# Where a rotary exchange runs: block 1's halves by DMAs of SyncE instead of TensorE, and three stack transfers by GpSimd's queue

## The chip, the core and the metric

The kernel runs on one core of a Trainium2 chip. The metric is the device time of one execution in microseconds; the time before the change is the median of three runs. A profile of one execution shows every instruction on TensorE (PE, with its weight loads PEld), VectorE (DVE), ScalarE (ACT), GpSimd (POOL) and the DMA queue of SyncE (SP). All times below are microseconds (us) from the start of the profiled span unless they are marked ns.

## The reference

`x` is 2 x 2048 x 256, float32. It is normalized over its last axis; the result feeds causal attention (16 heads of 16, 4 key and value heads) and a spectral layer; both are added to `x`.

```python
xn = _layernorm(x, axis=-1)
q = (xn @ wq).reshape(Bx, Sx, 16, 16); k = (xn @ wk)...; v = (xn @ wv)...
def _apply_rope(t, cos, sin):
    t1, t2 = jnp.split(t, 2, axis=-1)
    return jnp.concatenate([t1 * cos - t2 * sin, t1 * sin + t2 * cos], axis=-1)
q = _apply_rope(q, cos, sin); k = _apply_rope(k, cos, sin)
scores = jnp.where(causal, jnp.einsum('bshd,bthd->bhst', q, k) / sqrt(16), -inf)
out = jnp.einsum('bhst,bthd->bshd', softmax(scores), v).reshape(Bx, Sx, 256) @ wo
y = real(ifft(einsum('bnd,do->bno', fft(xn), w))) + bias
return x + out + y
```

What the change touches is `_apply_rope`: each half of a head's features is multiplied by the cosine, and the other half, exchanged, by the sine.

## The kernel before

The 2 x 2048 rows are cut into 8 blocks of 512 rows (`NB`), in the order block row 0 of both sequences, block row 1 of both, and so on: blocks 0 and 1 are the first 512 rows of the two sequences. Each block has 4 units of 4 heads, so 32 units in all; unit u of block n has the queries of 4 heads.

**Preparing a block** (`project`, lines 425 to 637). The rows are normalized (`norm`), transposed on TensorE (`ps_x`, copied to `xnT`) and multiplied with the weights (`features`, tile `ps_q`, copied by ScalarE to `raw`). This is done in three chunks of 128 features: `c == NK` (chunk 2 in the tile names) holds keys and values, chunks 0 and 1 the queries of units 0 and 1, and 2 and 3. Features of a head's two halves lie 32 partitions apart, so the exchange of halves (`other_half`, lines 486 to 511) moves groups of 32 partitions. For blocks 0 and 1 (`n < 2`) it is a TensorE product with a permutation (`swap`, tile `ps_sw`). Block 0's rotation runs on VectorE, which reads the product from PSUM. Block 1's runs on GpSimd from SBUF, so ScalarE copies the product to `sw` (line 501). From block 2 on, DMAs of SyncE copy `raw` to `sw` (lines 506 to 511): two for the keys, four for a query chunk.

`rotate` makes `raw * cos`, `sw * sin` and their sum, `split` cuts the float32 result into three bfloat16 parts "h", "m" and "l" (lines 579 to 609), on VectorE for block 0 and on GpSimd for the others (line 429). The parts are stacked on partitions into `kst` (keys) and `qst` (a unit's queries), by `QPART = "hmlhmhm"` in seven pieces of 64 KB. For keys and for the very first unit `stack` sends these seven directly (`direct`, line 529); for the other units `stack_runs` writes the parts to a buffer in DRAM (`run`) and reads the stack back in three transfers. All of these go through `later`, which puts them on SyncE's queue in one stream per block.

**The main loop.** For each unit the maxima of the score rows are taken first: TensorE computes scores (`sd` for the diagonal, `sm` for earlier blocks), VectorE reduces them (`top_g`, `mx`, then `np_of`, lines 686 to 815). `spread` (lines 817 to 830) turns the negated maxima by TensorE (`ps_m`), copies them on ScalarE to `mt`, and a DMA from ScalarE's queue appends them to the unit's `qst`. Only then can TensorE compute the transposed scores (`st`, or `sp` at the end), ScalarE their exponentials (`es`, line 952), and TensorE the product with the values (`av`). Later come the division by the sums and the output (`po`).

**What sets the order.** The order on every engine is written by the kernel's own planner while the kernel is built (lines 1344 to 1464). It keeps an estimated clock for each engine (`use`, line 127) and each DMA queue (`send`, line 141), with costs written into the code, and pieces of work in streams, each with what it needs and when it is due. It always takes the piece that its clocks say can start soonest, with preferences by kind (maxima, scores, values, fillers). Fillers are, among others, the six pieces of the spectral matrix (`spectral_matrix`, lines 361 to 410): four `ps_ff` and two `ps_mff`. Each engine then executes its instructions strictly in the planned order, waiting on semaphores. So a cost or a need that is changed in one place can move work anywhere.

Of the kernel before, what the change touches and what calls it, by code (L numbers as in the profile page):

```python
# [23 lines left out]
def tile_attn_plus_spectral_ffn(  # L24
# [29 lines left out]
    nc = tc.nc  # L54
# [3 lines left out]
    DH = 16  # L58
# [9 lines left out]
    NK = D // P  # L68
# [3 lines left out]
    QPART = "hmlhmhm"  # L72
# [20 lines left out]
    ring, used = {}, {}  # L93
# [6 lines left out]
    def take_slot(tag):  # L100
        used[tag] += 1
        return used[tag] - 1
# [24 lines left out]
    def use(eng, us, needs=(), gives=()):  # L127
        clock[eng] = max(clock[eng], ready(needs)) + us
        if eng == "pe":
            at = issued[0] // LOADED  # L130
            for k in range(max(loaded), at + 1):
                clock["pe"] = max(clock["pe"], loaded[k])
                loaded[k + 1] = clock["pe"] + LOAD
            clock["pe"] = max(clock["pe"], loaded[at])
        for k in gives:
            there[k] = clock[eng] + LATE[eng]
# [4 lines left out]
    def send(eng, kb, needs, gives, late=0.1):  # L141


        mine = lane.setdefault(eng == "pool", [0.0] * LANES)
        clock[eng] = max(clock[eng], mine[0])
        clock[eng] = max(clock[eng], ready(needs)) + (0.75 if eng == "pool" else 0.62)
        moved[eng] = max(moved.get(eng, 0.0), clock[eng] + 1.5) + 0.008 * kb
        mine.append(moved[eng] + 0.1)
        mine.pop(0)
        for k in gives:  # L150
            there[k] = moved[eng] + late
# [10 lines left out]
    def through_bank(us, needs, eng, eng_us, gives, eng_needs=()):  # L162

        k = take_slot("st")
        use("pe", us, (*needs, ("st", k - ring["st"])), [("ps", k)])
        use(eng, eng_us, (("ps", k), *eng_needs), [("st", k), *gives])
# [18 lines left out]
    def load_x(n):  # L185
# [31 lines left out]
        out=mask, in_=mask, pattern=[[-1, P]], compare_op=ALU.is_ge, fill=NEG, base=0,  # L217
# [6 lines left out]
        out=mask_t, in_=mask_t, pattern=[[1, P]], compare_op=ALU.is_ge, fill=NEG, base=0,  # L224
# [12 lines left out]
    for q in range(0, P, QD):  # L237
# [11 lines left out]
        out=rows_g[:, :, 0:3], in_=rows_g[:, :, 0:3], pattern=[[0, 2 * NKV], [-QD, 3]],  # L249
# [3 lines left out]
        out=rows_g[:, :, 38:41], in_=rows_g[:, :, 38:41], pattern=[[0, 2 * NKV], [QD, 3]],  # L253
# [48 lines left out]
    wp = const.tile([P, NK, NC, P], F32, name="wp")  # L302
# [122 lines left out]
    def project(n):  # L425
# [5 lines left out]
        raw, sw, swp, part, ra, at, held = {}, {}, {}, {}, {}, {}, {}  # L431
        sends = []
        streams.append(sends)

        def later(out, in_, kb, needs, gives):


            def go():
                nc.sync.dma_start(out=out, in_=in_)
                send("sp", kb, needs, gives)  # L440

            sends.append((-1, -1, "sp", needs, [], go))

        def norm(i):
            e.tensor_scalar(
# [19 lines left out]
        def features(c, k):  # L465
            if k == 0:
                held[c] = bank(f"ps_q{n}_{c}"), take_slot("st")
            ps, at_st = held[c]
            product(ps, wp[:, k, c, :], xnT[n][:, k, :], start=(k == 0), stop=(k == NK - 1))
            use("pe", 0.9, ["wp", ("xnT", n, k), ("st", at_st - ring["st"])], [("ps", at_st)])  # L470
            if k < NK - 1:
                return
            raw[c] = work.tile([P, SB], F32, tag="raw", bufs=3, name=f"raw{n}_{c}")
            at[c] = take_slot("raw")
            nc.scalar.copy(raw[c], ps)  # L475
            use(
                "act", 0.48, [("ps", at_st), ("raw", at[c] - ring["raw"])],
                [("st", at_st), ("raw", "in", n, c)],
            )
            if n >= 2:  # L480
                other_half(c)

        def rows(c):
# [2 lines left out]
        def other_half(c):  # L486
            sw[c] = work.tile([P, SB], F32, tag="sw", bufs=3, name=f"sw{n}_{c}")
            at[c, "sw"] = take_slot("sw")
            free = ("sw", at[c, "sw"] - ring["sw"])
            if n < 2:  # L490
                ps = bank(f"ps_sw{n}_{c}")
                product(ps, swap, raw[c], start=True, stop=True)
                if n == 0:
                    swp[c] = ps
                    at[c, "st"] = take_slot("st")
                    use(
                        "pe", 0.95, [("raw", "in", n, c), ("st", at[c, "st"] - ring["st"])],
                        [("sw", "in", n, c)],
                    )
                else:  # L500
                    nc.scalar.copy(sw[c], ps)
                    through_bank(
                        0.95, [("raw", "in", n, c)], "act", 0.48, [("sw", "in", n, c)], [free]
                    )
                return
            for base in range(0, rows(c), HP):
                one, two = slice(base, base + QD), slice(base + QD, base + HP)
                last = [("sw", "in", n, c)] if base + HP == rows(c) else []
                needs = [("raw", "in", n, c), free]
                later(sw[c][one, :], raw[c][two, :], 64, needs, [])  # L510
                later(sw[c][two, :], raw[c][one, :], 64, needs, last)
# [19 lines left out]
        def stack(c, a_part, f):  # L531
            src = part[c][f * HP : (f + 1) * HP, "hml".index(a_part), :]
            for a in range(len(QPART)):
                if (KPART if c == NK else QPART)[a] == a_part:
                    to = kst[n] if c == NK else qst[n, 2 * c + f]
                    gives = []
                    if a == len(QPART) - 1 if c == NK else a_part == "l":
                        gives = [("kst", n) if c == NK else ("stk", n, 2 * c + f)]
                        gives += [("part", at[c, "part"])] * (c == NK)
                    needs = [("part", "in", n, c, a_part)]  # L540
                    later(to[a * DH : (a + 1) * DH, :, :], src, 64, needs, gives)

        def stack_runs(c, units):

# [34 lines left out]
        def split(c, k):  # L579
# [23 lines left out]
            else:  # L603
# [7 lines left out]
        xs = [("xnT", n, k) for k in range(NK)]  # L611
        pe = [
            ("pe", [("xn", n, i) for i in range(NI)], ["st"] + ["xnT"] * (c == 0),
             lambda c=c: transpose_x(c))
            for c in range(NK)
        ]
        for c in (NK, 0, 1):
            table = [("cs", j, 1)] * (n >= 2)
            pe.append(("pe", ["wp", *table, xs[0]], ["st", "raw"] + ["sw"] * (n >= 2), lambda c=c: features(c, 0)))
            pe.append(("pe", [xs[1]], [], lambda c=c: features(c, 1)))  # L620
            if n < 2:
                pe.append(("pe", [("raw", "in", n, c)], ["st", "sw"], lambda c=c: other_half(c)))
            if c == NK:
                pe.append(("pe", [("raw", "in", n, NK), ("ones", n)], ["st"], proj_v))
# [572 lines left out]
    for u in range(len(units)):  # L1197
        at = max(0, first[u] - AHEAD[blocks[units[u][0]][1]])
# [317 lines left out]
```

## Time and profile before

| | |
|---|---|
| median of 3 runs | 898.05 us (897.0 to 899.27) |
| profiled execution, its time | 896.71 us |
| profiled execution, its span | 895.0 us |
| TensorE idle in the span | 895.0 - 879.4 = 15.6 us |
| `sw<-raw` DMAs | 60, 64 KB each |
| `res<-avs` issues of GpSimd's queue | 30, 600 ns each, 2.8 us to landing |

The span runs from the first instruction to the last; the execution's own time is 1.7 us longer. The page divides the span into 40 slices of 22.4 us; a digit is the busy share of a slice in tenths:

```profile
PE   8899999999999999999999999999999999999998
DVE  7987987798988996899888899979889889798501
POOL 8868558836932335611356321212652011101111
DMA  5554623441432012520012510010142001100000
```

TensorE is busy throughout. VectorE and GpSimd are as busy as TensorE only in the first 100 us, where blocks 0, 1 and 2 are prepared beside the first units. The granted TensorE clock was 1.0 throughout.

In the lists of instructions below each row gives the start, the length, the engine, the line, the operation, the tiles written and read, how many instructions were joined, and in brackets the idle time of the engine before it and what ended it. A product of the code is twice as many rows of float32 matmuls in the profile: the four matmuls of one `ps_sw` are eight rows.

### The profile page before, as it was taken

To read this page: it belongs to the slowest core of one execution; us is meant where nothing else is said; L and a number is where in the kernel's file an instruction comes from. 1 tells how busy PE (TensorE), PEld (TensorE's weight loads), DVE (VectorE), ACT (ScalarE), POOL (GpSimd) and SP (SyncE) were. 2 spreads that over 40 slices of the span, in tenths; PEclk is the share of its full clock that TensorE was granted. 3 is DMA by queue.
4 is the path that set the end of the run, shared out by engine and by line. 5 is a ranking of instruction groups with operands and counts; after the bars stand their busy time and mean duration, and the time that the engine had idled before them with its cause. 6 is when DMAs were issued, how large, how long until landed. Compare 5 with 4: busy or idle time off the path is not lost.

```text
span 895.0 us, 37152 instructions
## 1 busy us (share of the span) xinstructions
PE 879.4 (98%) x16620; PEld 481.8 (54%) x16620; DVE 730.8 (82%) x1002; ACT 638.3 (71%) x1191; POOL 365.0 (41%) x491
## 2 busy tenths in 40 slices
PE   8899999999999999999999999999999999999998
PEld 5477664565565555555555555554455554545443
DVE  7987987798988996899888899979889889798501
ACT  4276747685857874877855977858598887579885
POOL 8868558836932335611356321212652011101111
PEclk9999999999999999999999999999999999999999
DMA  5554623441432012520012510010142001100000
GB/s 176 139 137 118 197 67 112 123 120 49 107 106 86 27 40 78 142 74 15 17 44 87 150 40 14 27 39 14 52 123 61 14 3 39 50 14 15 27 2 25
DMA packets 42063, 62.02 MB, mean 69 GB/s; under 512 B 8920, under 2 KB 32200, under 8 KB 41904
## 3 DMA queue, kind: packets, MB, share of 16 engines
q1 hardware_dynamic: 32480, 41.18, 17.1%
q0 software_dynamic: 8128, 17.69, 6.2%
q8 instruction: 130, 2.13, 1.0%
q10 hardware_dynamic: 1296, 0.79, 0.3%
q14 instruction: 29, 0.24, 0.1%
HBM read 32.75 MB, written 18.40 MB: 57 GB/s over the span
## 4 chain that ended last, share of the span: by engine, by line
PE 88%; DVE 7%; ACT 3%; DMA 1%; issue 1%; SPq 0%; ACTq 0%; DVEq 0%
PE av L121 25%; PE st L121 24%; PE sm L121 18%; PE sd L121 7%; PE po L121 6%; PE ps_q L121 4%; ACT es L952 2%; DVE top_g L681 2%; PE sp L121 2%; DVE mx L681 1%; DMA qst<-mt 1%; PE ps_x L125 1%; PE ps_m L121 0%; DMA trig<-rope_dram 0%; DVE np_of L808 0%
## 5 line engine op out<-in xcount | busy, mean ns | idle before, releaser
L952 ACT ACTIVATE es<-st 128x512 f32<-128x512 f32 x1006 | 532.3, 605 | 133.6 <-PE st L121 116.9
L681 DVE TENSOR_REDUCE mx<-sm 128x2 f32<-128x1024 f32 x384 | 450.1, 1217 | 41.4 <-PE sm L121 40.0
L121 PE MATMUL st<-qst,kst 115*32 115x512 bf16 (+8 forms) x4744 | 340.5, 345 | 1.3 <-DMA qst<-mt 0.5
L121 PE MATMUL av<-es,va 128*32 128x512 f32 (+3 forms) x2560 | 289.7, 529 | 0.7 <-ACT avs L1033 0.2
L121 PE MATMUL sm<-kst,qst 112*32 112x512 bf16 x3072 | 237.9, 379 | 1.5 <-DVE top_g L681 0.8
L121 PEld LDWEIGHTS <-kst 115*32 115x32 bf16 x5120 | 164.2, 95 | 139.2 <-issue 62.3
L121 PEld LDWEIGHTS <-qst 112*32 112x32 bf16 x5632 | 153.2, 96 | 129.9 <-issue 82.1
L681 DVE TENSOR_REDUCE top_g<-sd 128x25 f32<-128x800 f32 (+1 forms) x192 | 167.5, 905 | 34.9 <-PE sd L121 34.5
L970 POOL TENSOR_SCALAR_AFFINE_SELECT es<-es 128x512 f32<-128x512 f32 (+1 forms) x120 | 65.3, 547 | 228.2 <-ACT es L952 228.2
L121 PEld LDWEIGHTS av<-es,va 128*32 128x32 f32 x2560 | 82.8, 109 | 47.4 <-issue 18.0
L121 PE MATMUL sd<-kst,qst 112*32 112x384 bf16 (+11 forms) x2560 | 101.1, 256 | 2.6 <-DVE top_g L681 1.7
L1044 POOL DMA_DIRECT2D res<-avs x30 | 18.0, 600 | 118.5 <-ACT avs L1023 118.5
L121 PEld LDWEIGHTS <-ident_h 128*32 128x32 bf16 x1344 | 46.2, 95 | 22.8 <-issue 16.3
L1158 DVE TENSOR_TENSOR xr<-po,xr 128x256 f32<-128x256 f32 x36 | 15.2, 424 | 47.1 <-PE po L121 46.7
L121 PE MATMUL sd<-mask,ident_h 128*32 128x64 bf16 x1024 | 53.4, 193 | 0.1
L121 PE MATMUL ps_q<-xnT,wp 128*32 128x512 f32 x384 | 47.5, 594 | 0.2 <-ACT xnT L460 0.2
L475 ACT COPY raw<-ps_q 128x512 f32<-128x512 f32 x24 | 14.1, 586 | 44.9 <-PE ps_q L121 37.1
L952 ACT ACTIVATE es<-sp 128x1024 f32<-128x1024 f32 x41 | 39.7, 1027 | 6.1 <-PE sp L121 5.9
L566 POOL TENSOR_TENSOR ra<-raw,cs 128x512 f32<-128x512 f32 (+1 forms) x21 | 27.0, 1286 | 24.6 <-ACT raw L475 23.6
L121 PE MATMUL po<-wo_sb,attT 128*32 128x256 f32 x512 | 34.4, 380 | 0.0
L121 PE MATMUL po<-mff,xnT 128*32 128x256 f32 x512 | 33.9, 379 | 0.0
L827 ACT CAST mt<-ps_m 12x512 bf16<-12x512 f32 x32 | 18.3, 571 | 19.1 <-PE ps_m L121 18.6
(113 smaller groups left out, 615.9 us busy)
## 6 DMA issues: line engine op xcount, KB each, us to landing
qst<-run SPq DMA_DIRECT2D x62, 128.0 KB
res<-avs POOLq DMA_DIRECT2D x30, 256.0 KB, 2.8
run<-part SPq DMA_DIRECT2D x31, 192.0 KB
qst<-run SPq DMA_DIRECT2D x31, 192.0 KB
xr<-in_L_attn_x_dram SPq DMA_DIRECT2D x16, 256.0 KB
sw<-raw SPq DMA_DIRECT2D x60, 64.0 KB
attT<-res POOLq DMA_DIRECT2D x15, 256.0 KB, 4.2
inv<-sums POOLq DMA_DIRECT2D x15, 256.0 KB, 3.7
```

The costliest lines, as they stand in the source:

```text
L121: nc.tensor.matmul(to, lhsT, rhs, **more)
L125: nc.tensor.transpose(to, of, unit)
L475: nc.scalar.copy(raw[c], ps)
L566: e.tensor_tensor(ra[c][:r], raw[c][:r], cs[j][:r, 0, :], ALU.mult)
L681: nc.vector.tensor_reduce(out, of, AX.X, ALU.max)
L827: nc.scalar.copy(mt, ps[0 : 3 * NKV, :SB])
L952: nc.scalar.activation(to, of, AF.Exp, scale=SCALE)
L970: nc.gpsimd.affine_select(out=to, in_=to, pattern=pattern, compare_op=ALU.is_ge, fill=0.0, base=0, channel_multiplier=-1,)
L1044: nc.gpsimd.dma_start(out=res[n, c][f], in_=avs[u])
L1158: nc.vector.tensor_tensor(xr[n, r][:, e, :], po, xr[n, r][:, e, :], ALU.add)
```

## The change

Block 1's exchange no longer goes through TensorE and ScalarE: it uses the same DMAs of SyncE as block 2 and later blocks, ten transfers of 64 KB for its three chunks. Only block 0 keeps the product. The features of block 1 accordingly ask for a free `sw` buffer before they start.

In the direct stack of the first unit, the three "h" pieces of the seven are issued from GpSimd's queue, in a stream of their own; the planner's note that the stack is complete (`stk`) then also needs those three. The key stacks (`c == NK`) stay on SyncE.

```diff
-        def later(out, in_, kb, needs, gives):
+        sends_pool = []
+        streams.append(sends_pool)
+
+        def later(out, in_, kb, needs, gives, pool=False):
+
+            q, name = (nc.gpsimd, "pool") if pool else (nc.sync, "sp")
 
             def go():
-                nc.sync.dma_start(out=out, in_=in_)
-                send("sp", kb, needs, gives)
-
-            sends.append((-1, -1, "sp", needs, [], go))
+                q.dma_start(out=out, in_=in_)
+                send(name, kb, needs, gives)
+
+            (sends_pool if pool else sends).append((-1, -1, name, needs, [], go))
...
-            if n >= 2:
+            if n >= 1:
                 other_half(c)
...
-            if n < 2:
+            if n == 0:
                 ps = bank(f"ps_sw{n}_{c}")
                 product(ps, swap, raw[c], start=True, stop=True)
-                if n == 0:
-                    swp[c] = ps
...
-                else:
-                    nc.scalar.copy(sw[c], ps)
-                    through_bank(
-                        0.95, [("raw", "in", n, c)], "act", 0.48, [("sw", "in", n, c)], [free]
-                    )
+                swp[c] = ps
...
                     needs = [("part", "in", n, c, a_part)]
-                    later(to[a * DH : (a + 1) * DH, :, :], src, 64, needs, gives)
+                    by_pool = c < NK and a_part == "h"
+                    if by_pool:
+                        gives = [("stk h", n, a)]
+                    elif gives and c < NK:
+                        needs += [("stk h", n, k) for k in range(7) if QPART[k] == "h"]
+                    later(to[a * DH : (a + 1) * DH, :, :], src, 64, needs, gives, by_pool)
...
-            pe.append(("pe", ["wp", *table, xs[0]], ["st", "raw"] + ["sw"] * (n >= 2), lambda c=c: features(c, 0)))
+            pe.append(("pe", ["wp", *table, xs[0]], ["st", "raw"] + ["sw"] * (n >= 1), lambda c=c: features(c, 0)))
             pe.append(("pe", [xs[1]], [], lambda c=c: features(c, 1)))
-            if n < 2:
+            if n == 0:
                 pe.append(("pe", [("raw", "in", n, c)], ["st", "sw"], lambda c=c: other_half(c)))
```

The transfers that are used instead were in the code already:

```python
            for base in range(0, rows(c), HP):
                one, two = slice(base, base + QD), slice(base + QD, base + HP)
                last = [("sw", "in", n, c)] if base + HP == rows(c) else []
                needs = [("raw", "in", n, c), free]
                later(sw[c][one, :], raw[c][two, :], 64, needs, [])
                later(sw[c][two, :], raw[c][one, :], 64, needs, last)
```

More of the change, by code (lines that the diff above doesn't have):

```diff
@@ L489, in other_half @@
             free = ("sw", at[c, "sw"] - ring["sw"])
-            if n < 2:
+            if n == 0:
                 ps = bank(f"ps_sw{n}_{c}")
                 product(ps, swap, raw[c], start=True, stop=True)
-                if n == 0:
-                    swp[c] = ps
[L495 to L498, printed above, removed]
-                    )
-                else:
-                    nc.scalar.copy(sw[c], ps)
-                    through_bank(
-                        0.95, [("raw", "in", n, c)], "act", 0.48, [("sw", "in", n, c)], [free]
-                    )
+                swp[c] = ps
+                at[c, "st"] = take_slot("st")
+                use(
+                    "pe", 0.95, [("raw", "in", n, c), ("st", at[c, "st"] - ring["st"])],
+                    [("sw", "in", n, c)],
+                )
                 return
```

## The prediction

> **What bounds the kernel now.** I read the page first (busy shares and the chain that ended last), then busy time by stretches, then the instructions of TensorE, VectorE and GpSimd between 14 and 100 us, and last the waits of the SyncE queue.
>
> ```profile
> span 895.0 us, 37152 instructions
> PE 879.4 (98%) x16620; PEld 481.8 (54%) x16620; DVE 730.8 (82%) x1002; ACT 638.3 (71%) x1191; POOL 365.0 (41%) x491
> ...
> PE 88%; DVE 7%; ACT 3%; DMA 1%; issue 1%; SPq 0%; ACTq 0%; DVEq 0%
> ```
>
> TensorE is the bound: 88% of the chain, and 895.0 - 879.4 = 15.6 us of idle in all. So a change is worth the TensorE work it removes, minus the TensorE idle it makes. The stretches (span; PE, PEld, DVE, ACT, POOL busy; clock; DMA share) say where the idle lies:
>
> ```profile
> 20.00:30.00 10.00, 9.31 (x144) 4.21 (x140) 9.55 (x14) 3.47 (x7) 9.25 (x14) 1.00 0.36 106
> 30.00:40.00 10.00, 8.41 (x188) 4.75 (x184) 8.93 (x16) 2.46 (x5) 8.48 (x8) 1.00 0.49 135
> 40.00:50.00 10.00, 9.01 (x274) 6.87 (x271) 9.18 (x26) 6.69 (x14) 9.42 (x12) 1.00 0.73 178
> 80.00:100.00 20.00, 18.62 (x580) 12.44 (x571) 17.73 (x38) 13.82 (x28) 17.44 (x21) 1.00 0.65 189
> 500.00:600.00 100.00, 100.00 (x1833) 53.91 (x1829) 88.46 (x101) 76.93 (x147) 19.64 (x30) 1.00 0.16 47
> ```
>
> About 8 us of idle lie before 100 us, 2.0 between 100 and 800, 5.6 at the end. The changed instructions all lie between 17 and 45 us, where VectorE and GpSimd are over 85% busy too. The gaps there, and one removed product, in TensorE's order of time (start, length, what, idle before it):
>
> ```profile
> 29.16 0.31 PE L121 MATMUL sd<-kst,qst 112*32 112x32 bf16 x8 [0.69 <-DMA qst<-part]
> ...
> 32.27 0.35 PE L121 MATMUL sd<-kst,qst 112*32 112x384 bf16 x4 [1.45 <-DVE top_g L681]
> ...
> 35.84 1.02 PE L121 MATMUL ps_sw<-raw,swap 128*32 128x512 f32 x5
> 36.65 1.94 PE L121 MATMUL ps_q<-xnT,wp 128*32 128x512 f32 x16
> ...
> 43.90 0.38 PE L121 MATMUL st<-qst,kst 115*32 115x512 bf16 x4 [0.52 <-DMA qst<-mt]
> ```
>
> The first gap is the wait for the stack the change touches, the second a wait for VectorE, the third the trip of the first unit's negated maxima (`mt`).
>
> **What goes away.** Three products `ps_sw` of block 1. Start to next start: 26.01 to 26.99, 35.79 to 36.65, 39.38 to 40.26: 0.98 + 0.86 + 0.88 = 2.7 us of TensorE. Their three ScalarE copies (586 ns each, 1.8 us) go too, worth nothing: ScalarE is busy 2.46 of 10 us at 30 to 40.
>
> **What SyncE gets.** Ten transfers `sw<-raw` more, three stack transfers fewer.
>
> ```profile
> L439 SPq DMA_DIRECT2D sw<-raw x60: 507/588/1216, 65.2 to 645.6; - x60
> ```
>
> At 0.6 us an issue that is 10 x 0.6 - 3 x 0.6 = 4.2 us more on an in-order queue. I replay it in its new order. Three "m" transfers 23.5 to 25.3, two `sw` of the key chunk (its `raw` is there at 25.2) to 26.5, the "l" transfer to 27.1, run 1 to 27.8, four `sw` of chunk 0 (28.6, after its `raw`) to 31.0, two of chunk 1 to 32.3, unit 1's three stack reads to 34.5 (32.27 before), two runs to 35.7, two `sw` to 36.9, five key transfers to 40.0, units 2 and 3 to 43.1, two key transfers to 44.3. With 2.2 us to land (the first pair of block 2's `sw` was issued by 66.4, its user started at 68.71), unit 0's stack is complete at 29.3, as now; unit 1's at 36.7, needed at about 39.2; block 1's keys at 46.5, needed at 65. So nothing on this queue reaches TensorE; without the 2.5 us of cover at unit 1 its lateness would count one for one. Later, units 6 and 7 stand behind block 2's first `sw` pair (issued near 67 instead of 59 to 65); their maxima come near 84 us.
>
> **What GpSimd gets.** Three issues of 0.6 us (`res<-avs`: 600 ns) after the key memset that ends at 23.17, so 23.2 to 25.0, landing near 27: before the "l" part. Block 1's key chunk starts at 25.2 instead of 25.97, but a 2.6 us memset pair now stands inside it, so its second step comes 1.4 us later than 27.79. Then
>
> ```profile
> 37.57 1.29 POOL L569 TENSOR_TENSOR sw<-sw,cs 128x512 f32<-128x512 f32 x1 [1.06 <-DVE top_g L681]
> ```
>
> this wait for chunk 0's exchange goes (the transfer lands by 33.2), which returns 1.06. GpSimd's chain is within 0.4 us of today's from there on.
>
> These three issues are the part for which I have no row: GpSimd's issues beside VectorE's casts. The nearest row is VectorE's cast, 0.44 us alone and 1.38 us beside a GpSimd multiply:
>
> ```profile
> 21.80 0.44 DVE L590 CAST part<-raw 128x512 bf16<-128x512 f32 x1
> ...
> 26.34 1.38 DVE L590 CAST part<-raw 128x512 bf16<-128x512 f32 x1
> ```
>
> Bounds: nothing, or one such 1.38 us hold for each issue, 4.1 us. I take nothing: only one 0.45 us cast (23.00) falls into 23.2 to 25.0, and the memset there did not stretch it. The Trainium skill, "SBUF — State Buffer", on the shared port pair, speaks against this part: a GpSimd-issued DMA needs GpSimd to write descriptors, which a VectorE copy in a two-port mode locks out, about 620 ns becoming 3100; by that figure the three would cost 7.4 us more (an estimate from that page), which no run here shows yet.
>
> **What the new order does.** Taking a need off TensorE lets the kernel's own planner choose anew, and this outweighs the rest. Six pieces of the spectral matrix (four `ps_ff`, two `ps_mff`, 1.73 us each: 3.49 for two) now all stand ahead of unit 0's `ps_m`; before, two did, two came later, and both `ps_mff` at 73.75. Replay of TensorE: `ps_ff` until 26.0, `ps_v` 26.4, chunks 0 and 1 at 1.73 each to 29.9, `ps_ff` 31.6, two diagonal steps of 0.4 to 32.4, `ps_ff` 34.1, two to 34.9, `ps_ff` 36.7, two to 37.4, `ps_mff` 39.2, two of unit 1 to 39.9, `ps_mff` 41.6, `ps_m`.
> 1. The gaps of 0.69 and 1.45 close: -2.1.
> 2. `ps_m` starts at 41.6 instead of 39.25. From it to the first `st` takes 43.90 - 39.25 = 4.65, so that comes at 46.25: 2.35 later. Only three diagonal steps (1.3 us) are left to cover that trip, so some 2.9 us are idle, against 0.52: +2.4.
> 3. From there to unit 1's first `st` it was 54.46 - 43.90 = 10.56 with one `ps_ff`, so 8.8 without: 55.1. But unit 1's `mt` must have landed: VectorE ends unit 0's maxima at 40.6 (last reduction 39.0, closing steps 1.6), then 2 x 0.7 + 4 x 0.95 + four statistics 2.4 + closing 1.5 make 49.7; a free bank and the steps ahead of it put `ps_m` at 50.9, ScalarE's copy ends at 52.0 behind its exponentials, 3.6 more (40.29 to 43.86) is 55.6. I take 55.6: 1.15 later than now.
> 4. The order is then the same until `ps_mff` at 73.75, which is done already: 1.15 - 3.49 = 2.3 us ahead. What VectorE does next, however, waits for its own chain: unit 4's maxima end at 76.5 + 1.15 = 77.65, and
>
> ```profile
> 77.81 5.14 DVE L681 TENSOR_REDUCE top_g<-sd 128x18 f32<-128x576 f32 x6 [1.32 <-PE sd L121]
> ```
>
> starts 0.16 earlier, no more. From here to 99.7 VectorE idles only 0.25 + 0.97 + 0.52 = 1.7, so the stretch ends between 0.16 and 1.9 us earlier. I take the middle, **1.0 us earlier**: 2.7 saved, 1.7 returned as idle.
> 5. After 100 us the order differs in most places but the work is the same, at 99.5 to 100% busy; the last units have the same order. Bounds: the 2.0 us of idle there vanish, or as much again comes; I take 0.
>
> Sum: 895.0 - 1.0 = 894.0 of span, 895.7 for the profiled execution (896.7); the median of the runs is 1.3 above that one, so 898.05 - 1.0 = **897.1 us**.
>
> **Rivals.**
> *Faster: the saving stays.* The 2.7 and the two closed gaps (2.1) count, and the late `mt` is covered by what VectorE and ScalarE have ready: 898.05 - 4.8 = 893.3; with only the 2.3 us of step 4 and half of the later idle, 894.8. For it: TensorE has almost no slack anywhere else, so work removed should show. Against it: VectorE's 17.7 of 20 us at 80 to 100. Center 894.
>
> *Slower: the trips of `mt` lose their cover.* With all fillers spent by 42 us, each unit of blocks 0 and 1 has only its own maxima, scores and values to cover some 4.2 us from `ps_m` to `st`. The planner counts 0.62 + 1.5 + 0.1 us for that transfer (lines 146 and 147), the trace 3.6 to 4.45. Six more trips follow before 100 us. Two of them as bare as step 2 (2.4 each) decide it: -1.0 + 4.8 = 901.9. For it: unit 2's trip (4.45 us from 59.93) is on the chain already. Against it: the orders after unit 1 are alike.
>
> *GpSimd held up.* At the 4.1 us bound the "h" parts land near 31.2, just before TensorE asks at 31.6, but block 1's chain on GpSimd is some 3.0 late, and block 2's normalization, now 2 us further back in its order, ends near 56 when TensorE wants it at 53.9: +2.2, 899.3. By the skill's figure above it would be worse still.
>
> That the products stay cannot be: they are gone from TensorE's order.
>
> **How the numbers follow.** Forecast 0.38, saving stays 0.32, bare trips 0.25, GpSimd held up 0.05. 0.3% is 2.7 us, about what a measurement of this kernel can tell from no change: limits 895.4 and 900.7. The forecast's own range is 895.0 to 899.0; 0.04 of it falls faster, 0.01 slower; of the last rival 0.02 slower. Faster 0.32 + 0.04 = 0.36, slower 0.25 + 0.01 + 0.02 = 0.28, same 0.36. Range: from 892.5 (4.8 and part of the later idle) to 902.5 (a third trip partly bare).
>
> **What would show it.** Right: no gap near 29 or 31 us, a wait `st <- DMA qst<-mt` of 2 to 3 us near 43 to 46, `top_g` of unit 5 near 77.7, PE busy 2 to 3 us less. Wrong: that wait under 1 us (faster), several such waits (slower), GpSimd's three issues over 1 us each, or waits of `sd` for `qst<-run`.

## The result, and the profile after

The changed kernel takes 895.39 us (median of 7 runs, 894.41 to 899.34) against 898.05: 0.9976 of the time before, 95% interval 0.9965 to 0.9988, some 2.7 us at the median. That lies on the border that the prediction itself drew between no change and faster (895.4). A second set of runs, further down, gives 895.79 and 0.9961 [0.9946, 0.9975]. The profiled execution took 896.04 us, with a span of 894.3. The head of its page and the chain that ended last:

```profile
span 894.3 us, 37136 instructions
PE 876.2 (98%) x16596; PEld 476.2 (53%) x16596; DVE 729.0 (82%) x1002; ACT 637.0 (71%) x1188; POOL 365.6 (41%) x494
...
PE 92%; DVE 5%; ACT 2%; issue 1%; DMA 0%; POOL 0%; ACTq 0%; POOLq 0%
```

TensorE has 24 matmuls (the three products) and 3.3 us of busy time less (879.4 before). Its idle time is 894.3 - 876.2 = 18.1 us, some 2.6 more than before. The span shrank by 0.7 only: 3.3 saved, 2.6 returned. The same stretches as shown of before (span; PE, PEld, DVE, ACT and POOL busy; clock; DMA share; GB/s) tell where:

```profile
20.00:30.00 10.00, 10.00 (x109) 3.96 (x105) 9.45 (x15) 3.56 (x7) 9.31 (x16) 1.00 0.39 94
30.00:40.00 10.00, 10.00 (x288) 7.25 (x284) 5.84 (x9) 1.98 (x5) 8.98 (x9) 1.00 0.65 161
40.00:50.00 10.00, 7.07 (x200) 4.76 (x189) 9.35 (x27) 4.07 (x10) 9.47 (x10) 1.00 0.50 134
80.00:100.00 20.00, 18.72 (x590) 12.92 (x584) 18.74 (x39) 15.21 (x30) 18.62 (x22) 1.00 0.63 171
500.00:600.00 100.00, 99.87 (x1811) 54.80 (x1807) 88.72 (x102) 74.53 (x143) 18.51 (x28) 1.00 0.11 33
```

The gaps at 20 to 40 us (0.7 and 1.6) are gone, and 1.9 us more are idle at 40 to 50. Over longer stretches, idle before and after: 7.9 and 9.0 up to 100 us, 3.5 and 3.4 from 100 to 885, 4.2 and 5.7 from there to the end. The timeline of TensorE shows the idle of 40 to 50 us (start, length, what, idle before it and its releaser):

```profile
41.91 0.22 PE L121 MATMUL ps_m<-ident_h,np_of 128*12 128x128 bf16 x1
...
45.01 0.35 PE L121 MATMUL sd<-kst,qst 112*32 112x384 bf16 x4 [1.92 <-DVE top_g L684]
...
46.46 0.38 PE L121 MATMUL st<-qst,kst 115*32 115x512 bf16 x4 [0.83 <-DMA qst<-mt]
...
55.35 0.38 PE L121 MATMUL st<-qst,kst 115*32 115x512 bf16 x4
```

Between unit 0's `ps_m` and its first `st` only a few diagonal steps are left, so TensorE waits once for VectorE to free a bank and once for the trip of `mt`: 2.75 us. From 38 to 60 us there is one wait more, to which the profile gives no releaser ("issue"); it ends at 59.3 us, and the experiments come back to it:

```profile
PE sd L121 <- issue: 0.7, 1, 0.7
```

In VectorE's timeline, unit 5's first reduction starts where it did before (77.81):

```profile
77.70 5.10 DVE L684 TENSOR_REDUCE top_g<-sd 128x18 f32<-128x576 f32 x6
```

From 77 to 100 us VectorE now hardly waits for scores any more; first before, then after (the columns: total, times, longest):

```profile
DVE top_g L681 <- PE sd L121: 3.1, 4, 1.3
```

```profile
DVE top_g L684 <- PE sd L121: 0.6, 1, 0.6
```

GpSimd's timeline has the three issues, at 0.54 us each, and no wait before chunk 0's `sw` step:

```profile
23.57 1.63 POOL L443 DMA_DIRECT2D qst<-part  x3
...
38.27 1.29 POOL L572 TENSOR_TENSOR sw<-sw,cs 128x512 f32<-128x512 f32 x1
```

How far is the changed kernel ahead? ScalarE's copy of `mt` marks each unit. Unit 0 starts it at 42.43 instead of 39.68, unit 1 at 51.47 instead of 49.52, unit 5 at 84.91 instead of 85.06, unit 7 at 99.60 instead of 101.03, unit 28 at 717.36 instead of 719.93, and the last unit is 2.43 us earlier, as is the last piece of computation. That is 1.7 us more than the span shows. The rest lies behind the last computation, in SyncE's wait for the output to land; first after, then before:

```profile
SPq L1515 <- DMA out_dram<-xr: 3.1, 2, 2.8
```

```profile
SPq L1512 <- DMA out_dram<-xr: 0.9, 2, 0.5
```

In this execution one packet of instructions (16 KB) ran at 890.9 to 891.85, and 18 packets of the output came in one by one until 892.9.

### The profile page after: what moved, and what is told of

Read it like the earlier page. It is cut to its first block, busy times and chain, and to the rows that moved or that the text cites. A ratio compares the mean times of both kernels' runs of the same rounds, so it can differ in the third digit from the quotient of the medians.

```text
span 894.3 us, 37136 instructions
## 1 busy us (share of the span) xinstructions
PE 876.2 (98%) x16596; PEld 476.2 (53%) x16596; DVE 729.0 (82%) x1002; ACT 637.0 (71%) x1188; POOL 365.6 (41%) x494
## 4 chain that ended last, share of the span: by engine, by line
PE 92%; DVE 5%; ACT 2%; issue 1%; DMA 0%; POOL 0%; ACTq 0%; POOLq 0%
PE av L121 25%; PE st L121 24%; PE sm L121 18%; PE sd L121 7%; PE po L121 6%; PE ps_q L121 5%; DVE top_g L684 2%; PE sp L121 2%; ACT es L955 1%; PE idle L125 1%; PE ps_x L125 1%; DVE mx L684 1%; PE ps_ff L121 1%; DVE np_of L811 1%; PE ps_m L121 1%
## 5 line engine op out<-in xcount | busy, mean ns | idle before, releaser
L121 PEld LDWEIGHTS <-qst 112*32 112x32 bf16 x5632 | 150.4, 96 | 127.3 <-issue 81.9
L1072 POOL DMA_DIRECT2D sums<-den x15 | 8.0, 534 | 63.7 <-DVE den L1066 63.7
```

What stands on the lines that cost most here:

```text
L121: nc.tensor.matmul(to, lhsT, rhs, **more)
L1072: nc.gpsimd.dma_start(out=sums, in_=den[n, c])
```

## The experiments

Ratios are to runs of the kernel before on the same chip. A lead or lag of two kernels with the same order was read at the same matmul of TensorE, counted from the start.

**1. The parts, and the order.** The change does three things at once: it takes the products away, it moves three issues to GpSimd, and it lets the planner choose a new order. Four kernels take these apart. The first keeps the order of the kernel before and only puts DMAs in the place of the products:

```diff
 if n < 2:
-    ps = bank(f"ps_sw{n}_{c}")
-    product(ps, swap, raw[c], start=True, stop=True)
     if n == 0:
+        ps = bank(f"ps_sw{n}_{c}")
+        product(ps, swap, raw[c], start=True, stop=True)
...
-        nc.scalar.copy(sw[c], ps)
...
+        for base in range(0, rows(c), HP):
...
+            nc.sync.dma_start(out=sw[c][one, :], in_=raw[c][two, :])
+            nc.sync.dma_start(out=sw[c][two, :], in_=raw[c][one, :])
```

> Block 1's exchange by DMAs, but every engine keeps the order of the kernel before (the planner still counts the three products; they are only not emitted, and the DMAs stand at their place in SyncE's queue); the stack stays whole on SyncE. If removed TensorE work counts wherever it stands (rival), all 2.7 us show: 895.4. Mine: in the old order the products stand in stretches whose end is set by VectorE (unit 0's maxima) and by the trip of mt, so unit 0's first st stays near 43.9 us and most of the 2.7 turns into waits of sd and st there; 897 to 898, lead over the kernel before under 1 us.

899.74 us, 1.0006 [0.9994, 1.0017]: nothing gained. It starts well: at 42 to 48 us (times of the kernel before at the same matmul) it is 1.7 to 2.5 us ahead. Then comes one wait of TensorE, and the queue of SyncE shows why:

```profile
PE sd L121 <- DMA qst<-run: 3.3, 1, 3.3
```

```profile
42.39 0.58 SPq L439 DMA_DIRECT2D qst<-run  x1
...
44.93 1.89 SPq L505 DMA_DIRECT2D sw<-raw  x1
46.86 5.39 SPq L439 DMA_DIRECT2D qst<-run  x5
```

One of six stack reads of units 2 and 3 is issued at 42.4; the other five stand behind the four transfers of the exchange and start at 46.9. Behind the wait the kernel is 1.3 us late, from 53 us on 2.8, and from 60 us on 4.0. The last two steps are not the queue. In the first of them TensorE's granted clock is 0.5 from 51.06 to 54.47 us, which the stretch from 46 to 55 us shows as a mean of 0.81 (span; PE, PEld, DVE, ACT, POOL busy; clock; DMA share; GB/s):

```profile
46.00:55.00 9.00, 5.37 (x105) 3.27 (x104) 4.43 (x14) 1.61 (x4) 8.75 (x12) 0.81 0.42 112
```

Whether the wait for the queue set this off is not shown. The second step is a wait without a releaser, which ends at 63.95 us (part 4 shows what such waits are):

```profile
PE sd L121 <- issue: 1.0, 1, 1.0
```

My expectation that the saving would hardly show at unit 0 was wrong, and the time lies above the expected 897 to 898: the saving showed, and the queue turned it into a lag of 1.3 us, to which the halved clock and the wait added 2.7.

The second has the exchange by DMA in the planner's own order, with all seven stack transfers left on SyncE:

```diff
-by_pool = c < NK and a_part == "h"
+by_pool = False
...
-elif gives and c < NK:
+elif False:
```

> Only the exchange of block 1 by DMAs, the planner free to choose anew; all seven stack transfers of the first unit on SyncE. Mine: the saving is the removed work plus the new order, not GpSimd's three issues, so within 1.5 us of the changed kernel: 894 to 897. Rival (the stack transfers by GpSimd are what makes it pay, since SyncE's queue else delays the first unit's stack by two pairs of sw): 897.5 or slower, with a wait of the first sd for qst<-part.

894.71 us, 0.9951 [0.9938, 0.9964]: the whole gain. The third has the GpSimd part alone, with the products:

```diff
+            q, name = (nc.gpsimd, "pool") if pool else (nc.sync, "sp")
...
+                    by_pool = c < NK and a_part == "h"
-                    later(to[a * DH : (a + 1) * DH, :, :], src, 64, needs, gives)
+                    later(to[a * DH : (a + 1) * DH, :, :], src, 64, needs, gives, by_pool)
```

> Only the three h transfers by GpSimd's queue; block 1's exchange stays on TensorE. Mine: no TensorE work goes, the planner only deals its pieces anew: 898 plus or minus 1.5. Rival (the gain is a luckier order, whatever set it off): 895.5 or faster.

897.2 us, 0.9978 [0.9965, 0.9992]. It too gets an order of its own from the planner, and its compute ends 0.6 us before that of the kernel before, so this run doesn't tell the issues from the order. It holds all the products and is still 1.7 us faster at the medians than the kernel before, by ratio as much as the first set of the changed kernel (0.9976). So an order dealt anew can be worth that much alone; what the removed products add shows beside it on the same chip, where the exchange alone reached 0.9951 and the two intervals do not meet. The fourth has the order of the changed kernel, but TensorE's products and ScalarE's copies in the places where the exchange's DMAs were issued:

```diff
+            def by_product():
+                ps = bank(f"ps_sw{n}_{c}")
+                for q in range(0, P, QD):
+                    nc.tensor.matmul(ps[q : q + QD], swap[:, q : q + QD], raw[c], start=True, stop=True)
+                nc.scalar.copy(sw[c], ps)
...
-                later(sw[c][two, :], raw[c][one, :], 64, needs, last)
+                later(
+                    sw[c][two, :], raw[c][one, :], 64, needs, last,
+                    instead=n == 1 and (by_product if last else (lambda: None)),
+                )
```

> The changed kernel's plan and order, but block 1's exchange is computed by the three products and ScalarE copies after all, each emitted where the chunk's last exchange transfer stood; no exchange transfers for block 1. The order is kept and only the 2.7 us of TensorE work come back. If the removed work is what the gain consists of (mine), the time rises by 2 to 2.7 over the changed kernel, to 897.5 to 898. If the new order alone brought the gain (rival), it stays at 895.4.

898.82 us, 1.0003 [0.9989, 1.0016]: the time before, 0.8 above what I expected; the profiled execution took 897.58. So neither the exchange in the old order nor this new order with the products is worth anything; both together are worth 2.7 to 3.3 us at the medians. The page of the fourth kernel:

```profile
PE 879.0 (98%) x16620; PEld 476.6 (53%) x16620; DVE 728.8 (81%) x1002; ACT 638.3 (71%) x1191; POOL 365.4 (41%) x494
```

TensorE is busy 879.0 us against 876.2: the products are 2.8 of the 3.3 us saved.

**2. Is it the queue?** Two kernels keep the old order as the first did, but start the last four exchange transfers elsewhere:

```diff
-nc.sync.dma_start(out=sw[c][one, :], in_=raw[c][two, :])
-nc.sync.dma_start(out=sw[c][two, :], in_=raw[c][one, :])
+queue = nc.gpsimd if c == 1 else nc.sync
+queue.dma_start(out=sw[c][one, :], in_=raw[c][two, :])
+queue.dma_start(out=sw[c][two, :], in_=raw[c][one, :])
```

> The order of the kernel before with the exchange by DMAs, as in the run that kept the order, but the four transfers of the last piece of block 1 (128 rows) start on GpSimd's queue instead of ahead of unit 1's transfers on SyncE's. Theory (in the run that kept the order the removed work was given back in SyncE's queue): TensorE's wait of 3.3 us for unit 1's features falls below 1.0, unit 2 starts as far ahead as unit 1, and the whole takes 895.5 to 897.0, 2 to 3 less than that run. Rival (the order of before can't use the freed time, whichever queue carries the exchange): 898.5 or more, with another wait of 2 us or more before unit 4.

The second has `nc.scalar` in the place of `nc.gpsimd`.

> The same with those four transfers on ScalarE's queue, behind the copy that makes their source. Theory: 895.5 to 897.5; ScalarE issues for some 2.4 us there (four at the 0.6 us that SyncE's took), so what it copies next for unit 1 comes up to 2.4 us later, and the wait of 3.3 us falls all the same. Rival: 898.5 or more, as with GpSimd's queue, or more than that where ScalarE's copies are late.

On GpSimd's queue: 900.7 us, 1.0029 [1.0014, 1.0044], 3.7 us above the range of the theory. On ScalarE's queue: 897.8 us, 0.9991 [0.9979, 1.0003], 0.3 above the range of the theory. TensorE's waits, first with GpSimd's queue, then with ScalarE's between 38 and 60 us:

```profile
PE sd L121 <- DVE top_g L686: 2.5, 3, 2.0
PE sd L121 <- DMA qst<-run: 1.8, 1, 1.8
```

```profile
PE sd L121 <- DMA qst<-run: 1.8, 1, 1.8
PE st L121 <- ACT at__348 L382: 1.2, 1, 1.2
```

The wait of 3.3 us falls to 1.8, not below 1, and another of 2.0 or 1.2 stands beside it. GpSimd issues from 44.68 to 46.76 ahead of its own cast, so what it prepares for block 1 comes 3.7 us later than in the first run (2.1 of them the issues); ScalarE issues from 40.30 to 42.87 ahead of its copy of `ps_ff`. All three kernels are 1.6 to 2.0 us ahead at 43 us; at 60 us they are 4.0, 4.6 and 0.9 late, and at the last matmul 3.3 and 3.4 late and 0.4 ahead. But these three profiles differ in the clock too. Here is the stretch from 46 to 55 us with GpSimd's queue, then with ScalarE's:

```profile
46.00:55.00 9.00, 5.45 (x100) 3.19 (x101) 3.23 (x11) 1.75 (x4) 8.61 (x11) 0.81 0.52 125
```

```profile
46.00:55.00 9.00, 6.97 (x188) 4.84 (x184) 6.64 (x19) 3.50 (x8) 8.75 (x12) 1.00 0.74 179
```

With GpSimd's queue the granted clock is 0.5 from 48.52 to 51.93 us, and the lag grows by some 1.4 us there; with ScalarE's queue it stays at 1.0. So the queue was only the first of several places in which the old order gives the saved time back. The times of two queues of three agree with the rival (the old order can't use it), but those are the two whose profiles have the halved clock, so the order is not shown as the only cause.

**3. The gap at 40 to 50 us.** If the new order loses 2.4 us there by spending its fillers too soon, holding them back should win them. This kernel is the changed one with the last fillers tied to later steps:

```diff
+            at_needs = ["neg_s"] + [("s", 3)] * (o == 1)
+            et_needs = ["neg_s"] + [("s", 1)] * (o == 0)
...
-            pieces.append((lefts, lambda r=r: right(r)))
+            pieces.append(([*lefts, ("mt", "out", 0, 0)], lambda r=r: right(r)))
```

> The changed kernel, but the last three ps_ff are let go only when VectorE has taken unit 0's second and fourth diagonal step, and the two ps_mff only when unit 0's mt is on its way, so that they cover that trip. Theory of the prediction (fillers spent too early return 1.7 of the 2.7 us as idle): unit 0's mt comes 2 to 3 us earlier than in the changed kernel, the wait st for qst<-mt goes, and compute ends 1 to 2 us earlier: 893.5 to 894.5. Rival (VectorE's chain and the arrival of instruction pages bound the first 100 us, so the lead is eaten there): the mt of unit 0 comes earlier, but at unit 8 the lead is within 0.5 us of the changed kernel's, and the time within 0.7 of 895.4.

898.51 us, 0.9998 [0.9989, 1.0006]: both expectations missed. The edit did its work: unit 0's copy of `mt` starts at 39.83, 2.6 us earlier than in the changed kernel. But unit 1 starts at 50.76 (51.47), unit 5 at 85.06 (84.91) and unit 7 at 99.33 (99.60): of the 2.6 us 0.3 are left after 100 us. From there on the planner's order is another one, and the kernel ends 3.6 us later at 3.7 us more TensorE busy time for the same instructions. So by 100 us the early gap has cost next to nothing here, and what an order is worth later is not read from the early stretch.

**4. The end, and places without a cause.** Two kernels are the changed one with 24 small matmuls more (48 instructions of TensorE with their weight loads), written to an unused part of a bank: behind unit 0's `ps_m`, where TensorE idles, and behind `ps_a` of unit 30. The kernel of the first test:

```diff
+            if n == 0 and g == 0:
+                for _ in range(24):
+                    nc.tensor.matmul(ps[64 : 64 + QD, 0:QD], ident_h[:, 0:QD], ident_h[:, 0:QD], start=True, stop=True)
```

> The changed kernel with 24 small bfloat16 matmuls more behind unit 0's ps_m (48 TensorE instructions with their weight loads, the number that the change took away), in the idle time before sd; they feed nothing. In the profile of the changed kernel the last compute ended 2.4 us earlier than before, but the last output landed 1.7 us later after it, and a packet of the instruction queue lay in that time (890.9), which before lay ahead of the last outputs (887.9). If the count of TensorE instructions sets when that packet is fetched and the packet holds up the output (mine), the drain is back to 2.7 us after SyncE's last issue and the time falls by 1.5 to 893.9. If the slow drain is chance or has another cause, the time stays at 895.4, or is up to 0.5 slower by the added matmuls.

And of the second:

```diff
+        for _ in range(24):
+            nc.tensor.matmul(spare[64 : 64 + QD, 0:QD], ident_h[:, 0:QD], ident_h[:, 0:QD], start=True, stop=True)
```

> The changed kernel with the 24 spare matmuls behind ps_a of the second last unit (near 865 us), where TensorE has room beside ScalarE: all before it is as in the changed kernel, and the last instruction packet must come ahead of the last outputs again. Drain theory: compute ends 2.0 to 2.4 us before that of the old kernel and SyncE's wait for the last output is under 1 us instead of 2.8; the time is 1.0 to 1.7 below the changed kernel's, 893.7 to 894.4. If the long drain has another cause, it stays 2.8 us and the time 895.4 or a little more.

896.67 us, 0.9971 [0.9958, 0.9983], and 896.96 us, 0.9987 [0.9976, 0.9998]. Both profiles have the short end again (0.5 us for the longest wait of SyncE in the second), but neither kernel is faster, and both times lie above what either side had expected: the late matmuls themselves cost 1.4 us, and the kernel with the early ones lost more elsewhere. Then came the changed kernel once more, beside the one with the exchange alone on the same chip:

> The changed kernel once more, beside the next one on the same chip. Theory (removed TensorE work is the gain; the three transfers on GpSimd's queue are worth nothing; the last packet of instructions lands beside the output, since its place in the stream is fixed): 895.2 to 896.0, ratio to before near 0.997, the last packet again later than 890.5 and the drain from TensorE's last start near 5.7 us. Rival (the late packet is chance): 893.7 to 894.5, the last packet near 888 and a drain near 4.0 to 4.3.

> The exchange by DMA alone, all seven transfers on SyncE's queue, once more beside the changed kernel. Theory: 0.5 to 1.7 us less than the changed kernel of the same call (what the drain costs that one), with the compute ending at the same time within 0.3 us. Rival (the part on GpSimd's queue is worth something and the first comparison, of two sessions, misled): equal to the changed kernel within 0.3 us or slower.

895.79 us, 0.9961 [0.9946, 0.9975], and 895.87 us, 0.9960 [0.9948, 0.9973]: equal, so the three issues on GpSimd's queue are worth nothing that can be seen, and the 894.71 of the first set was not a better kernel. The time of the changed kernel is the one that the theory gave, its end is the rival's: in the second profile the wait is short, so the long one belongs to one execution:

```profile
SPq L1515 <- DMA out_dram<-xr: 0.9, 2, 0.5
```

That execution lost its time at other places, with the same instructions in the same order: 0.6 us up to 30 us, and 1.25 us at the trip of unit 0's `mt` (here the timeline at the first `st`):

```profile
48.30 0.58 PE L121 MATMUL st<-qst,kst 115*32 115x512 bf16 x4 [2.08 <-DMA qst<-mt]
```

2.08 us instead of 0.83. Some 0.9 us more went right behind it, where the granted clock was 0.5 from 48.18 to 51.59 us; the stretch from 46 to 55 us in this execution, then in the first:

```profile
46.00:55.00 9.00, 6.83 (x196) 4.73 (x192) 5.98 (x17) 4.75 (x9) 7.97 (x11) 0.81 0.66 160
```

```profile
46.00:55.00 9.00, 8.26 (x240) 5.64 (x243) 8.54 (x24) 6.26 (x13) 8.67 (x13) 1.00 0.56 142
```

At unit 7 it is 2.7 us behind the first profile and 1.2 behind the kernel before, and its last computation ends 0.6 us after that of the kernel before. So one profile is no better than some 3 us in this stretch.

The early padding is the more telling one. Its order is that of the changed kernel, as is the order with the products back, and both shift what follows by 24 matmuls. Lag behind the changed kernel at the same matmul, by the time of that one:

```
us in the changed kernel     62.7   89.9   98.8   99.6  113.6  122.8  732.4
products back                0.82   0.84   1.12   2.26   2.60   2.78   3.05
early padding               -0.81  -0.80  -0.79   0.88   0.87   1.37   2.14
```

With the products back the kernel is 2.5 us behind at 43 us. It regains 0.9 at unit 0's `mt`, for which it need not wait, and 0.8 near 59 us, where the changed kernel itself stands still for 0.7 us. Between 63 and 98 us hardly anything lasts in either. Then both lose time at the same instructions near 99, from 114 to 123 and between 123 and 732 us, the padded kernel 2.9 us in all, though there it has no work that the changed kernel doesn't have. In the waits of TensorE from 95 us on the largest show as "issue", an idle engine that waits for nothing in the profile; the padding up to 105 us, then the products up to 125:

```profile
PE av L121 <- issue: 1.5, 1, 1.5
```

```profile
PE av L121 <- issue: 0.9, 1, 0.9
PE st L121 <- issue: 0.3, 1, 0.3
```

The profile counts 130 packets of instructions of 16 KB each; 33,192 instructions of TensorE by 130 is 255, so I take a packet for 256 instructions and call it an instruction page. The stalls sit just behind such a packet (one ends at 98.89 us in the kernel with the exchange alone, which stalls 1.48 us from 98.83 on), and at one count of instructions whatever stands there. Measured from the start of the last matmul to that of the next, they are: after the 4264th with the exchange alone (1.48 and 1.26 us in its two profiles), with the padding (1.68) and with the products back (1.15), which have another order; after the 4519th or 4521st in others, 255 to 257 further.

All the profiles together say the same. Between 40 and 885 us, the 14 of them hold 26 waits of TensorE of 0.18 us or more without a releaser. In each the work goes on 1.2 to 1.5 us behind the end of a 16 KB packet, and each lies at one of seven counts: near 1966, 3754, 4264, 4520, 4775, 5286 and 25,992, which are whole numbers of steps of 255 to 256 apart. The changed kernel's own stall near 59 us is the first of these. To test this, 24 instructions more were put into the warm-up of the kernel with the exchange alone:

```diff
-    for _ in range(48):
+    for _ in range(44):
...
+    for _ in range(16):
+        nc.tensor.matmul(idle[0:QD, 0:QD], ident_h[:, 0:QD], ident_h[:, 0:QD], start=True, stop=True)
```

> The kernel of the exchange alone (e2) with 24 TensorE instructions more in the warm-up: four transposes less, 16 small matmuls more, about the same time. Every later instruction's number rises by 24, nothing else changes. Page theory: gaps of TensorE that nothing explains lie at the same instruction numbers as in e2 and e4 (4264 within a few), now at work that is 24 instructions earlier, and follow an instruction packet; the time changes by what these gaps change, 893.5 to 896. Rival (the gaps belong to the work): they stay at the same matmuls, at numbers 24 higher, and the time is that of e2, 894.7.

896.25 us, a little above the expected range, and 0.9976 [0.9966, 0.9985], against 0.9951 and 0.9960 for the kernel without the 24. At 88 us it is 0.37 behind, at 114 us 1.84, at 733 us 2.44; the stall after the 4264th instruction stayed at the 4264th, 24 instructions earlier in the program, and one of 1.48 us came after the 4775th, 511 further. The waits for "issue", first of the shifted kernel, then of the first profile without the shift:

```profile
PE st L121 <- issue: 3.3, 4, 1.3
```

```profile
PE st L121 <- issue: 1.7, 2, 1.2
```

That the stalls follow the instruction pages is shown by these; that the medians differ by as much is likely, not shown, since the second profile of the unshifted kernel has also a stall after the 4775th (0.99 us) and its interval overlaps.

## Why the prediction was right or wrong

The forecast, 897.1 us with 895.0 to 899.0 as its own range, is 1.7 us above the result, which lies inside the whole range and between the forecast and the rival that the saving stays (894). The forecast gain was 1.0 us, the measured one 2.7. The places named below are those of the first profile; in the second one unit 0's first `st` started at 48.30, and unit 7 stood 1.2 us behind the kernel before, so the close agreement of the early steps is in part luck. The steps, one by one:

- *Removed work, 2.7 us.* Right: the products are 879.0 - 876.2 = 2.8 us of busy time with the order held fixed.
- *SyncE's replay: nothing reaches TensorE.* Right in the order that the planner chose, which has no wait for `qst<-run` above 0.2 us, though the replay ran ahead of the queue: the six reads of units 2 and 3 were issued until 48.2 us, not 43.1. The runs that kept the old order show what the cover is worth: there the same ten issues cost a wait of 3.3 us at once.
- *GpSimd's issues, taken at nothing.* Right: 0.54 us each, below the 0.6 of the row that I used, and the cast beside them took 0.45 us. (GpSimd's chunk 0 step came at 38.27 instead of 37.57, 0.7 later where I had allowed 0.4; no wait of TensorE from 20 to 100 us ends on GpSimd.) The Trainium skill, "SBUF — State Buffer", on the shared port pair, would have made them 7.4 us more (an estimate from that page's figure); the trace shows none of it, and the pair of runs on one chip agrees.
- *Steps 1 to 3.* Right, to 0.3 us: the gaps near 29 and 31 us are gone; `ps_m` at 41.9 (41.6 foretold), unit 0's first `st` at 46.46 (46.25), 2.75 us idle (2.9), unit 1's first `st` at 55.35 (55.6). One detail was off: 1.9 of the 2.75 us are a wait for VectorE, not for the `mt` DMA.
- *Step 4, VectorE holds the lead back.* Right as far as the first profile shows. `top_g` of unit 5 came at 77.70 (77.65 foretold), VectorE's waits for scores from 77 to 100 us fell from 3.1 to 0.6 us, and the lead at unit 7 is 1.43 us, inside the bounds of 0.16 and 1.9; I took 1.0. The gap that was shifted by 2.6 us left 0.3, which agrees. The products that were put back do not bear on it: they counted only 0.8 to 1.1 us up to 98 us, but what they lost on the way went at unit 0's `mt` and at the changed kernel's own stall near 59 us.
- *Step 5, nothing after 100 us.* This is the step that failed. The lead grew by another 1.0 us, from 1.43 to 2.43, while the idle between 100 and 885 us stayed the same (3.5 and 3.4). I had bounded this stretch by its idle alone. What the runs showed in its place: the stretch is open to time that the order and the offset of the instructions move, 2 to 3 us here. With the products back in the same order, 1.9 us were lost after 98 us, 1.2 of them at stalls behind instruction pages, and the padding lost 2.9 there without any product, 2.6 of them at such stalls.

So the 2.4 us by which the last computation comes earlier in these profiles have three parts: about 1 us of the removed work up to 98 us; some 2 us because the changed stream does not lose after 98 us what the same order with 24 matmuls more does lose, 1.2 of them at stalls; less 0.6 us by which that order, with the products and the stalls, ends later than the kernel before. The middle part is the best founded: both profiles of the changed kernel, and the one with the late padding up to its padding, have no stall behind an instruction page after 98 us. The others rest on one profile each and are a split, not a proof. Why the kernel before, with as many instructions in another order, shows no such stall, and where within 100 to 885 us its TensorE is 1.0 us slower, stays open.

The last term of the sum, from the span to the median, was off too: the sum was made against a profiled execution 1.3 us below its median, and the one after lies 0.65 above its own, with its end longer by 1.7 us than before. The span says 0.7 us gained, the medians 2.7, the last computation 2.4.

Of the rivals, the bare trips of `mt` did not come in the first profile, where one trip is short of cover, with 0.8 us of such waits in all; in the second there were two, with 2.7 us, and its time is 1.8 above its median. GpSimd was not held up. *The saving stays* came nearest, but not by its reasons: most of the early lead was given back as the forecast says, 0.4 us more than forecast was left at 100 us, and the rest came behind it.

## What to carry to other kernels

Work removed from the busiest engine is worth what the order can use: the same 2.8 us were worth nothing that could be measured in the old order, where waits for the queues, a halved clock and a stall took them back, and 2.7 to 4.2 at the medians with an order planned anew, which alone was worth 0 in one case and 1.7 in another. So try a saving with and without the planner before judging it. Look at the granted clock of the very stretch before you blame a queue or an order for it. For effects below 0.5%, hold the order and shift the instruction stream of the bounding engine by a few dozen instructions before you name a cause, and compare two kernels at the same instruction, not by their spans. Profile the same kernel twice: here one execution differed from another by 3 us in the first 100 us, and by 1.5 at its end.

## What the runs showed of the hardware

- TensorE's instructions come in pages of 256 (130 packets of 16 KB for 33,192 instructions), one every 4.3 to 5.1 us by that count where it runs 50 to 59 instructions a microsecond, as in most stretches from 40 to 100 us. In that dense stretch it stalled 0.2 to 1.8 us at some page ends up to 120 us, and the work went on 1.2 to 1.5 us behind the end of the packet. At 500 to 600 us, with 36 a microsecond (1811 matmuls and 1807 loads in 100 us), it hardly stalled at all (0.13 us idle), though three profiles have a stall of 0.2 to 0.7 us near 678 us, always after the 25,990th to 25,994th instruction. The Trainium skill, "Runtime: NRT & Kernel Launch", in its section on instruction fetch, has the same blocks of 16 KiB and 256 instructions and calls the cost of a crossing "mostly hidden"; the size agrees, and in the dense stretch the measurement does not.
- In four of the 14 profiles TensorE's granted clock fell to 0.5 for 3.41 us in the midst of its work, once, between 46.5 and 54.5 us, within 1 us of the end of a wait of TensorE of 0.9 to 3.3 us. A row of `st` matmuls, four bfloat16 ones that start 512 columns wide, then took 0.58 us instead of 0.38. The waits alone do not decide it: the kernel with the late padding had it behind waits of 1.92 and 0.91 us, the changed kernel behind 1.92 and 0.83 did not.
- The same 12 KB transfer of `mt`, with the same instructions around it, kept TensorE waiting 0.83 us in one execution and 2.08 in another.
- The last output took 2.8 us of waiting in one execution and 0.5 in another of the same kernel. In the first a packet of instructions ran from 1.5 to 2.5 us behind the end of the last computation, and the last packet of the output came 3.5 us behind it. In the second the packet of instructions ended within 0.2 us of that end, and the last output came at 2.0. In six other profiles that packet was over at least 0.6 us before the end of the computation, and the last output came at 1.5. So the end goes with the place of that packet; that the packet is the cause is not shown, and only one profile has the long end.
